# A state-space mixer with a gated FFN on one core: another start for the LayerNorm and the first FFN step

## The chip, the cores and the metric

The kernel runs on one core of a Trainium2 chip. The metric is the device time of one execution in microseconds (us), taken as the median of several runs; lower is better. TensorE (PE in the profile) multiplies matrices, VectorE (DVE) and ScalarE (ACT) work elementwise, GpSimd (POOL) casts weights here and issues some DMAs, SyncE (SP) issues most DMAs. Each engine takes its instructions in the order of the program and waits on semaphores for the others.

## The reference, cut to what matters

The input has 1024 tokens (4 batches of 256) of 512 features. They are normalised once, and two branches read the result:

```python
xn = (x - mean(x)) / sqrt(var(x) + 1e-5)          # per token, over 512 features
s  = mixer(xn)                                    # projections, convolution, decayed state sums, gate, out projection
h  = silu(xn @ gate_w.T) * (xn @ up_w.T)          # FFN, 512 -> 1792
g  = silu(h @ down_w.T)                           # 1792 -> 512
out = x + s * g
```

FFN weights are integers in {-1, 0, 1} with one scale per row. The mixer is by far the larger part.

## The kernel before

Tokens are cut into eight tiles `t` of 128 (`xts[t]`, 128 tokens on the partitions by 512 features). A tile is normalised in place and then turned by TensorE (four 128x128 transposes, `ln_turn`) so that features lie on the partitions. The turned tile is copied by ScalarE into `xnT` (`keep`), which the mixer reads. For the FFN it is also split into a high part `xh` (rounded to the fast matmul type, ScalarE) and a low part `xl` (the rest, VectorE) by `split_tile`; a product with `xh` and one with `xl` together have full precision.

All of the change lies in `front`, which takes the first 300 us of the span. Its main loop runs over 28 FFN steps `(h, f)`: two halves `h` of 512 tokens by 14 tiles `f` of 128 FFN channels. Tiles 0 to 3 are half 0. A step issues, in this order: the loads of a later step's weights (`load_ffn`, three DMAs of 256 KB on SP's queue); the gate product `pg` (eight matmuls of 128x512, `project_exact`); its Silu `sg` on ScalarE; the up product `pu` (eight matmuls); `sg` times `pu` on VectorE (line 584); the next step's weight casts from integer to the matmul type on POOL (`cast_ffn`); the high part `hh` (ScalarE, line 592) and the low part `hl` (VectorE, line 596) of the product; and, two steps late, the down product `pf` (eight matmuls, `down_next`).

Between these calls each step takes three turns of `pieces`, a hand-written list of other work that fills the engines: `first_pieces` normalises and turns tiles 4 to 7, then forms sums of `xnT` for the mixer; from turn 6 on `dt_pieces` runs beside it (two products `pd` of the step sizes, `dt_project(0)` over half 0 and two turns later `dt_project(1)` over half 1, and softplus work); from turn 11 on come the mixer's B and C projections. Nothing is reordered by a scheduler: each engine's order is the order in which the program issues. A tile pool with n buffers makes a new tile wait until the tile n before it is no longer read. Tiles 4 to 7 are turned in a PSUM pool with one buffer (`ps_t`), so a turning waits for the `keep` of the turning before it.

Before the loop, the program loads tiles 0 to 3, step 0's weights, tiles 4 to 7, step 1's weights and small constants, issues eight matmuls `idle` that nobody reads (`busy(8)`), and then walks tiles 0 to 3 in a staggered order:

```python
for t in range(5):
    if t < 4:
        ln_stats(t)
        ln_std(t)
    if t:
        nc.vector.reciprocal(rstd[:, t - 1:t], rstd[:, t - 1:t])
        ln_norm(t - 1)
        tps.append(ln_turn(t - 1))
        busy(4)
    if t > 1:
        split_tile(xh, xl, t - 2, tps[t - 2])
split_tile(xh, xl, 3, tps[3])
```

`ln_stats` is two VectorE instructions (statistics and aggregate), `ln_std` a square root on ScalarE, followed by a reciprocal on VectorE. ScalarE holds one table of functions at a time: Sqrt and Silu are in different tables, and a change of table is an instruction of its own in the profile (ACT_TABLE_LOAD).

Of the kernel before, what the change touches and what calls it, by code (L numbers as in the profile page):

```python
# [43 lines left out]
F32 = mybir.dt.float32  # L44
F32R = mybir.dt.float32r
I32 = mybir.dt.int32
AF = mybir.ActivationFunctionType
ALU = mybir.AluOpType
PSUM = bass.MemoryType.PSUM

P = 128
# [4 lines left out]
NT = T // P  # L56
HID = 512
KT = HID // P
# [3 lines left out]
G = 8  # L62
# [3 lines left out]
CT = DIN // P  # L66
# [7 lines left out]
EPS = 1e-5  # L74
LEAD = 10
EARLY = 10
HALF = T // 2
# [5 lines left out]
def mixer_ffn(ctx: ExitStack, tc: tile.TileContext, x, in_w, conv_w, conv_b, dt_bias, a_log, d_col,  # L83
              norm_w, out_w, gate_t, up_t, down_t, gate_s, up_s, down_s, out):
    nc = tc.nc

    const = ctx.enter_context(tc.tile_pool(name="const", bufs=1))
    small = ctx.enter_context(tc.tile_pool(name="small", bufs=3))
    dram = ctx.enter_context(tc.tile_pool(name="dram", bufs=1, space=bass.MemoryType.DRAM))
    ps_proj = ctx.enter_context(tc.tile_pool(name="ps_proj", bufs=3, space=PSUM))  # L90
# [5 lines left out]
    eps = const.tile([P, 1], F32, name="eps")  # L96
# [5 lines left out]
    tiny = const.tile([P, 1], F32, name="tiny")  # L102
# [29 lines left out]
    def load_w(*tiles):  # L132
        w = wp.tile([P, 2, KT, P], F32, name="w")
        for n, i in enumerate(tiles):
            nc.sync.dma_start(w[:, n], in_w[i])
        return w
# [18 lines left out]
    def combine_w(w):  # L155
        s = scp.tile([P, 3, KT // 2, P], F32, name="s")
        for _ in combine_to(s[:, 0], s[:, 1], s[:, 2], blocks(w)[2], w):
            pass
        return factors(w, s)
# [34 lines left out]
    def front(pre, one_of, fp, f2, hp, ep):  # L194
# [14 lines left out]
        bias = one_of.tile([P, 1], F32, name="bias")  # L209
# [4 lines left out]
        steps = [(h, f) for h in range(2) for f in range(FT)]  # L214
        loads = {}

        def load_ffn(n):
            f, ts = steps[n][1], []
            for tag, src in (("wg", gate_t[f]), ("wu", up_t[f]),
                             ("wd", down_t[f * P:(f + 1) * P, :])):  # L220
                wi = f2.tile([P, HID], I32, name=f"{tag}_i", tag=f"{tag}_i")
                nc.sync.dma_start(wi, src)
                ts.append((tag, wi))
            loads[n] = ts
# [12 lines left out]
        def load_x(ts):  # L237
            for t in ts:
                xt = pre.tile([P, HID], F32, name="xt")
                nc.sync.dma_start(xt, x[t * P:(t + 1) * P, :])  # L240
                xts.append(xt)

        mv = one_of.tile([P, NT, 2], F32, name="mv")
        rstd = one_of.tile([P, NT], F32, name="rstd")
        nc.scalar.activation(rstd[:, 0:1], eps, AF.Sqrt)

        def ln_stats(t):
            st = small.tile([P, 6], F32, name="st")
            nc.vector.bn_stats(st, xts[t])
            nc.vector.bn_aggr(mv[:, t, :], st)  # L250

        def ln_std(t, n=1):
            nc.scalar.activation(rstd[:, t:t + n], mv[:, t:t + n, 1], AF.Sqrt, bias=eps)

        def ln_norm(t):
            nc.vector.tensor_scalar(xts[t], xts[t], mv[:, t, 0:1], rstd[:, t:t + 1],
                                    ALU.subtract, ALU.mult)

        def ln_turn(t):

            p, tag = ((ps_o, "o"), (ps_y, "y"))[t // 2] if t < 4 else (ps_t, "t")
            tp = p.tile([P, KT, P], F32, name="tp", tag=tag)
            for k in range(KT):
                nc.tensor.transpose(tp[:, k, :], xts[t][:, k * P:(k + 1) * P], ident)
            return tp

        def keep(t, tp):
            nc.scalar.copy(xnT[:, :, t * P:(t + 1) * P], tp)

        def busy(n):  # L270

            for _ in range(n):
                nc.tensor.matmul(idle, ones, ones, start=True, stop=True)
# [4 lines left out]
        def split_x():  # L278
            return [hp.tile([P, KT, HALF], F32R, name=n) for n in ("xh", "xl")]

        def split_tile(xh, xl, t, v):
            to = slice(t % 4 * P, (t % 4 + 1) * P)
            nc.scalar.copy(xh[:, :, to], v)
            nc.vector.tensor_tensor(xl[:, :, to], v, xh[:, :, to].bitcast(F32), ALU.subtract)

        def project_exact(w, xh, xl):
            pp = ps_proj.tile([P, HALF], F32, name="pp", tag="proj")
            for k in range(KT):
                for part in (xh, xl):
                    nc.tensor.matmul(pp, w[:, k * P:(k + 1) * P], part[:, k, :],  # L290
                                     start=(k == 0 and part is xh),
                                     stop=(k == KT - 1 and part is xl))
            return pp
# [24 lines left out]
        held = {}  # L318
# [69 lines left out]
        def combine_x(n):  # L388

            a, b = ((x12, x11), (x22, xc[:, 0]), (x22, x12), (x21, xc[:, 1]))[n]  # L390
            nc.vector.tensor_sub(xc[:, n], a, b)

        def first_pieces():
            for t in range(4, NT):
                ln_stats(t)
                if t % 2:
                    yield
            ln_std(4, 4)
            nc.vector.reciprocal(rstd[:, 4:], rstd[:, 4:])
            ln_norm(4)  # L400
            yield
            ln_norm(5)
            yield
            for t in range(4, NT):
                if t + 2 < NT:
                    ln_norm(t + 2)
                keep(t, ln_turn(t))
                yield
            yield
            for n in range(4):  # L410
                combine_x(n)
                if n == 0:
                    held["a"] = combine_w(held.pop("w"))
                yield
# [113 lines left out]
        load_ffn(0)  # L528
        nc.sync.dma_start(gs, gate_s)
        nc.sync.dma_start(us, up_s)  # L530
        load_x(range(4, NT))
        load_ffn(1)
        nc.sync.dma_start(wdt, in_w[PROJ // P - 1])
        nc.sync.dma_start(bias, dt_bias)
        nc.sync.dma_start(a_neg, a_log)
        for to, src in ((cw, conv_w), (cb, conv_b), (dcol, d_col), (nw, norm_w)):
            nc.sync.dma_start(to, src)
        nc.sync.dma_start(ds_bc, down_s.partition_broadcast(P))
        held["w"] = load_w(2 * CT + G, 2 * CT)

        idle = ps_t.tile([P, P], F32, name="idle", tag="t")
        xh, xl = split_x()
        busy(8)
        ws, tps = cast_ffn(0), []
        for t in range(5):
            if t < 4:
                ln_stats(t)
                ln_std(t)
            if t:
                nc.vector.reciprocal(rstd[:, t - 1:t], rstd[:, t - 1:t])  # L550
                ln_norm(t - 1)
                tps.append(ln_turn(t - 1))
                busy(4)
            if t > 1:
                split_tile(xh, xl, t - 2, tps[t - 2])
        split_tile(xh, xl, 3, tps[3])
        for t in range(4):
            keep(t, tps[t])
        pending = []

        def down_next():
# [6 lines left out]

        pfs = None
        for n, (h, f) in enumerate(steps):  # L570
            if n + 2 < len(steps):
                load_ffn(n + 2)
            pg = project_exact(ws[0], xh, xl)
            sg = fp.tile([P, HALF], F32, name="sg")
            nc.scalar.activation(sg, pg, AF.Silu, scale=gs[:, f:f + 1])
            if f == 2 and h:
                ffn_out(h - 1, pfs, (2, 3))
            next(pieces, None)
            pu, wd = project_exact(ws[1], xh, xl), ws[2]
            if f == FT - 1 and h == 0:  # L580
                xh, xl = split_x()
                for t in range(4, NT):
                    split_tile(xh, xl, t, xnT[:, :, t * P:(t + 1) * P])
            nc.vector.scalar_tensor_tensor(sg, pu, us[:, f:f + 1], sg, ALU.mult, ALU.mult)
            if n + 1 < len(steps):
                ws = cast_ffn(n + 1)
            next(pieces, None)
            if len(pending) == 2:
                down_next()
            hh = fp.tile([P, HALF], F32R, name="hh")  # L590
            hl = fp.tile([P, HALF], F32R, name="hl")
            nc.scalar.copy(hh, sg)
            if f == 1 and h:
                ffn_out(h - 1, pfs, (0, 1))
            next(pieces, None)
            nc.vector.tensor_tensor(hl, sg, hh.bitcast(F32), ALU.subtract)
            pending.append((f, hh, hl, wd))
        w = load_w(1, CT + 1)
# [6 lines left out]

    with (tc.manual_schedule(), tc.tile_pool(name="pre", bufs=NT) as pre,
          tc.tile_pool(name="one_of", bufs=1) as one_of, tc.tile_pool(name="fp", bufs=3) as fp,
          tc.tile_pool(name="f2", bufs=2) as f2, tc.tile_pool(name="hp", bufs=1) as hp,
          tc.tile_pool(name="ep", bufs=3) as ep):
        a, w = front(pre, one_of, fp, f2, hp, ep)  # L610

# [211 lines left out]
    with tc.manual_schedule():  # L823
# [4 lines left out]
        for i in range(CT):  # L828
# [32 lines left out]
            if 0 < i < CT - 1:  # L861
                w = load_w(i + 1, CT + i + 1)
# [206 lines left out]
        for n in range(2):  # L1069
            two, to = slice(2 * n, 2 * n + 2), slice(n * HALF, (n + 1) * HALF)  # L1070
# [3 lines left out]
        for n in range(2):  # L1074
            to = slice(n * HALF, (n + 1) * HALF)
# [97 lines left out]
```

## Time and profile before

| | |
|---|---|
| median of 3 runs | 1718.75 us (1718.47 to 1719.07) |
| profiled execution, time | 1718.77 us |
| profiled execution, span from first to last instruction | 1717.1 us |
| PE busy in the span | 1707.1 us |
| DVE, ACT, POOL busy | 1448.4, 1071.3, 217.1 us |
| mean granted TensorE clock | 1.000 |
| first matmul of the FFN starts at | 12.63 us |

The profiled execution's time is its span and 1.67 us around it. Start times are counted from the span's first instruction. A row of the timeline gives the start, the time taken, the engine and line, the operation, what it writes and reads, and in square brackets how long the engine had been idle before it and whom it waited for. The ends of matmuls are modelled, so the pitch between the starts of neighbouring matmuls says more than the time of one.

### The profile page before, as it was taken

The page shows a single profiled execution, that of the slowest core. Times are in us where ns is not written, and L with a number is a line of the kernel's source. Part 1 is how long each engine was busy: PE and PEld are TensorE (multiplying, and loading weights), DVE is VectorE, ACT ScalarE, POOL GpSimd, SP SyncE. Part 2 cuts the span into 40 slices and gives each one's busy share as a digit, 9 for nine tenths or more (in the row PEclk, how much of TensorE's full clock was granted, in tenths as well). Part 3 has the DMA queues.
Part 4 walks back from the last instruction along what each step waited for, and adds up shares of the span by engine and source line. Part 5 has one row for each costly group of instructions (what it writes and reads, how often), then busy time and mean ns, then how long its engine had stood idle before and what let it go on. Part 6 is the DMA issues. An engine that isn't in the chain of part 4 may idle for free.

```text
span 1717.1 us, 22516 instructions
## 1 busy us (share of the span) xinstructions
PE 1707.1 (99%) x8458; PEld 1098.8 (64%) x8458; DVE 1448.4 (84%) x1742; ACT 1071.3 (62%) x1439; POOL 217.1 (13%) x238
## 2 busy tenths in 40 slices
PE   8999999999999999999999999999999999999999
PEld 6666667555566666666666666666666666666687
DVE  5769787788888898889888988898889888899876
ACT  4554333688866666666766676667666666667640
POOL 3223323000000000111011101010111010101110
PEclk9999999999999999999999999999999999999999
DMA  6347665576766666777676767776776676667775
GB/s 227 93 166 251 209 237 201 205 222 209 238 203 205 198 215 175 201 201 205 184 207 197 214 189 211 206 217 194 212 204 203 193 209 195 197 183 210 207 215 182
DMA packets 161931, 347.27 MB, mean 202 GB/s; under 512 B 15136, under 2 KB 52896, under 8 KB 161824
## 3 DMA queue, kind: packets, MB, share of 16 engines
q1 hardware_dynamic: 139136, 292.89, 49.5%
q0 software_dynamic: 22688, 52.96, 17.5%
q8 instruction: 67, 1.10, 0.3%
q14 instruction: 40, 0.33, 0.1%
HBM read 236.48 MB, written 81.00 MB: 185 GB/s over the span
## 4 chain that ended last, share of the span: by engine, by line
PE 96%; DVE 2%; DMA 1%; ACT 0%; issue 0%; SPq 0%; ACTq 0%
PE px L175 29%; PE po L783 22%; PE pq L175 14%; PE py L702 10%; PE pz L175 7%; PE pp L290 5%; PE tp L658 3%; PE pf L298 2%; PE pg L478 1%; DVE cT L183 1%; DMA ya<-gated 0%; PE pd L326 0%; DMA wdt<-in_in_w 0%; DMA wd_i<-in_down_t 0%; DMA w<-in_in_w 0%
## 5 line engine op out<-in xcount | busy, mean ns | idle before, releaser
L175 PE MATMUL px<-xc,w 128*128 128x512 f32 x576 | 271.3, 593 | 0.0
L183 DVE SCALAR_TENSOR_TENSOR xT<-xpad,cw,xT 128x1024 f32<-128x1024 f32 x192 | 246.1, 1282 | 10.0 <-ACT xT L179 5.7
L191 DVE TENSOR_TENSOR_SCAN m<-m,after 128x1024 f32<-128x1024 f32 x108 | 246.4, 2281 | 0.0
L783 PE MATMUL po<-wo,ya 128*128 128x256 f32 x768 | 176.5, 379 | 0.0
L652 DVE TENSOR_TENSOR m<-m,gm 128x1024 f32<-128x1024 f32 x128 | 150.6, 1218 | 15.0 <-ACT m L644 15.0
L702 PE MATMUL py<-m,v 128*64 128x128 f32 x2048 | 160.7, 276 | 0.0
L921 POOL DMA_DIRECT2D sqacc<-sq x54 | 46.1, 853 | 869.5 <-ACT sq L917 805.4
L783 PEld LDWEIGHTS po<-wo,ya 128*128 128x128 f32 x768 | 141.5, 190 | 17.1 <-issue 0.2
L175 PE MATMUL pz<-xnT,w 128*128 128x512 f32 x288 | 145.8, 592 | 0.0
L175 PEld LDWEIGHTS px<-xc,w 128*128 128x128 f32 x576 | 99.3, 190 | 72.2 <-issue 68.9
L175 PE MATMUL px<-xnT,w 128*128 128x512 f32 x288 | 141.8, 615 | 0.0
L175 PE MATMUL pq<-xnT,s 128*128 128x512 f32 x288 | 136.1, 595 | 0.3 <-DVE xpad L951 0.3
L175 PE MATMUL px<-xc,s 128*128 128x512 f32 x288 | 135.7, 593 | 0.6 <-ACT cpad L441 0.5
L175 PE MATMUL pq<-xc,s 128*128 128x512 f32 x288 | 135.3, 592 | 0.0
L644 ACT ACTIVATE m<-m 128x1024 f32<-128x1024 f32 x128 | 134.3, 1058 | 0.6
L658 PEld LDWEIGHTS tp<-ident,xT 128*128 128x128 f32 x512 | 67.8, 141 | 99.4 <-issue 87.6
L702 PEld LDWEIGHTS py<-m,v 128*64 128x64 f32 x2048 | 117.7, 137 | 20.3 <-issue 19.1
L783 PE MATMUL po<-tw,sy 128*128 128x256 f32 x512 | 115.9, 379 | 0.0
L783 PEld LDWEIGHTS po<-tw,sy 128*128 128x128 f32 x512 | 97.2, 190 | 13.2
L891 ACT COPY gT<-px 128x512 f32<-128x512 f32 x64 | 37.5, 586 | 106.0 <-PE px L175 103.1
L702 PE MATMUL py<-mo,v 128*64 128x128 f32 x1024 | 99.7, 273 | 0.0
L175 PEld LDWEIGHTS pq<-xc,s 128*128 128x128 f32 x288 | 54.7, 190 | 68.9 <-issue 62.0
(189 smaller groups left out, 3106.5 us busy)
## 6 DMA issues: line engine op xcount, KB each, us to landing
m<-rows SPq DMA_DIRECT2D x108, 512.0 KB, 6.5
w<-in_in_w SPq DMA_DIRECT2D x144, 256.0 KB, 6.8
mo<-rows SPq DMA_DIRECT2D x128, 256.0 KB, 7.4
gated<-yg SPq DMA_DIRECT2D x64, 512.0 KB, 8.4
ya<-gated SPq DMA_DIRECT2D x30, 1024.0 KB, 7.2
sqacc<-sq POOLq DMA_DIRECT2D x54, 512.0 KB, 6.3
wo<-in_out_w SPq DMA_DIRECT2D x64, 256.0 KB, 6.8
acc<-sa POOLq DMA_DIRECT2D x23, 512.0 KB, 6.0
```

The costliest lines, as they stand in the source:

```text
L175: nc.tensor.matmul(pp, a[:, k, :], b[:, k, :], start=start and k == 0, stop=k == KT // 2 - 1, skip_group_check=not start)
L183: nc.vector.scalar_tensor_tensor(xT, xpad[:, :, k:k + L], cw[:, i, k:k + 1], xT, ALU.mult, ALU.add)
L191: nc.vector.tensor_tensor_scan(m, m, after, 0.0, ALU.add, ALU.mult)
L290: nc.tensor.matmul(pp, w[:, k * P:(k + 1) * P], part[:, k, :], start=(k == 0 and part is xh), stop=(k == KT - 1 and part is xl))
L298: nc.tensor.matmul(pf, part[:, i * P:(i + 1) * P], wd, start=(f == 0 and part is hh), stop=(f == FT - 1 and part is hl))
L644: nc.scalar.activation(m, m, AF.Exp)
L652: nc.vector.tensor_mul(m, m, gm[:, 0:T])
L658: nc.tensor.transpose(tp[:, b, :], xT[:, b, c * P:(c + 1) * P], ident)
L702: nc.tensor.matmul(py[d, q * P:(q + 1) * P], v[:, b, h, :], m, start=False, stop=True, skip_group_check=True)
L783: nc.tensor.matmul(po, a[:, k, :], b[:, k, :], start=start and k == 0, stop=k == HG - 1, skip_group_check=not start)
L891: nc.scalar.copy(gT[:, HALF:], px)
L921: nc.gpsimd.dma_start(sqacc, sq, accum_op=ALU.add)
```

## The change

Six edits, all in `front`:

- Tiles 0 to 3 are normalised one after the other on VectorE before any `xl`; the turnings are issued after that, with `idle` matmuls 12, 4, 4, 2, 2 where there were 8, 4, 4, 4, 4. The Silu table is loaded right after the four `xh`, and two of the four `keep` copies are issued after step 0's Silu.
- Step 0 multiplies the high parts of gate and up first (four and four matmuls) and then the low parts, into two PSUM banks.
- Tiles 4 to 7 get the inverse root on VectorE: a first value from the bits of the number and three Newton steps, twelve instructions on 128x4 elements, for one Sqrt on ScalarE and one reciprocal.
- The turnings of tiles 4 to 7 come one turn later (turns 5 to 8 for 4 to 7); an empty turn behind them goes, so that what follows keeps its turns.
- Weights are loaded three steps ahead for two (`f2` has three buffers for two).
- The order of the first DMAs: step 1's weights before tiles 4 to 7, then step 2's weights, then the mixer's first weight tile `held["w"]`, then the constants.

```diff
-        def ln_std(t, n=1):
-            nc.scalar.activation(rstd[:, t:t + n], mv[:, t:t + n, 1], AF.Sqrt, bias=eps)
+        def ln_std(t):
+            nc.scalar.activation(rstd[:, t:t + 1], mv[:, t, 1:2], AF.Sqrt, bias=eps)
+
+        def ln_inverse(t):
+            nc.vector.reciprocal(rstd[:, t:t + 1], rstd[:, t:t + 1])
...
+        def rstd_begin(to, v):
+            nc.vector.tensor_scalar(v, v, EPS, None, ALU.add)
+            bits = to.bitcast(I32)
+            nc.vector.tensor_scalar(bits, v.bitcast(I32), 1, None, ALU.logical_shift_right)
+            nc.vector.tensor_scalar(bits, bits, -1, 0x5f375a86, ALU.mult, ALU.add)
+
+        def rstd_refine(to, v):
+            y2 = small.tile([P, NT // 2], F32, name="y2")
+            nc.vector.scalar_tensor_tensor(y2, to, -0.5, to, ALU.mult, ALU.mult)
+            nc.vector.tensor_mul(y2, y2, v)
+            nc.vector.scalar_tensor_tensor(to, y2, 1.5, to, ALU.add, ALU.mult)
...
+        def project_part(pp, w, part, first):
+            for k in range(KT):
+                nc.tensor.matmul(pp, w[:, k * P:(k + 1) * P], part[:, k, :],
+                                 start=first and k == 0, stop=not first and k == KT - 1)
...
-            ln_std(4, 4)
-            nc.vector.reciprocal(rstd[:, 4:], rstd[:, 4:])
+            to, v = rstd[:, 4:], mv[:, 4:, 1]
+            rstd_begin(to, v)
+            for _ in range(3):
+                rstd_refine(to, v)
             ln_norm(4)
             yield
             ln_norm(5)
+            yield
             yield
             for t in range(4, NT):
                 if t + 2 < NT:
                     ln_norm(t + 2)
                 keep(t, ln_turn(t))
                 yield
-            yield
...
+        load_ffn(1)
         load_x(range(4, NT))
-        load_ffn(1)
+        load_ffn(2)
+        held["w"] = load_w(2 * CT + G, 2 * CT)
...
-        held["w"] = load_w(2 * CT + G, 2 * CT)
...
-        busy(8)
+        busy(12)
+        for t in range(4):
+            ln_stats(t)
+            ln_std(t)
+            if t:
+                ln_inverse(t - 1)
+                ln_norm(t - 1)
+        ln_inverse(3)
+        ln_norm(3)
         ws, tps = cast_ffn(0), []
...
         for t in range(4):
+            tps.append(ln_turn(t))
+            busy(4 if t < 2 else 2)
+            split_tile(xh, xl, t, tps[t])
+        nc.scalar.activation(tiny, eps, AF.Silu)
+        for t in range(2):
             keep(t, tps[t])
+        first = [proj_bank() for _ in range(2)]
+        for part in (xh, xl):
+            for pp, w in zip(first, ws):
+                project_part(pp, w, part, part is xh)
...
-            if n + 2 < len(steps):
-                load_ffn(n + 2)
-            pg = project_exact(ws[0], xh, xl)
+            if n + 3 < len(steps):
+                load_ffn(n + 3)
+            pg = project_exact(ws[0], xh, xl) if n else first[0]
             sg = fp.tile([P, HALF], F32, name="sg")
             nc.scalar.activation(sg, pg, AF.Silu, scale=gs[:, f:f + 1])
+            if n == 0:
+                for t in range(2, 4):
+                    keep(t, tps[t])
...
-            pu, wd = project_exact(ws[1], xh, xl), ws[2]
+            pu, wd = project_exact(ws[1], xh, xl) if n else first[1], ws[2]
...
-          tc.tile_pool(name="f2", bufs=2) as f2, tc.tile_pool(name="hp", bufs=1) as hp,
+          tc.tile_pool(name="f2", bufs=3) as f2, tc.tile_pool(name="hp", bufs=1) as hp,
```

More of the change, by code (lines that the diff above doesn't have):

```diff
@@ L284, in split_tile, with proj_bank @@
             nc.vector.tensor_tensor(xl[:, :, to], v, xh[:, :, to].bitcast(F32), ALU.subtract)
+        def proj_bank():
+            return ps_proj.tile([P, HALF], F32, name="pp", tag="proj")
+        def project_part(pp, w, part, first):
+            for k in range(KT):
+                nc.tensor.matmul(pp, w[:, k * P:(k + 1) * P], part[:, k, :],
+                                 start=first and k == 0, stop=not first and k == KT - 1)
         def project_exact(w, xh, xl):
-            pp = ps_proj.tile([P, HALF], F32, name="pp", tag="proj")
+            pp = proj_bank()
             for k in range(KT):
@@ L538, in front @@
         nc.sync.dma_start(ds_bc, down_s.partition_broadcast(P))
-        held["w"] = load_w(2 * CT + G, 2 * CT)
         idle = ps_t.tile([P, P], F32, name="idle", tag="t")
         xh, xl = split_x()
-        busy(8)
-        ws, tps = cast_ffn(0), []
[L545 to L556, printed above, removed]
-        for t in range(4):
+        busy(12)
[7 more added lines that the diff above has]
+        ln_norm(3)
+        ws, tps = cast_ffn(0), []
+        for t in range(4):
+            tps.append(ln_turn(t))
[3 more added lines that the diff above has]
+        for t in range(2):
             keep(t, tps[t])
+        first = [proj_bank() for _ in range(2)]
+        for part in (xh, xl):
+            for pp, w in zip(first, ws):
+                project_part(pp, w, part, part is xh)
         pending = []
```

## The prediction

> **What bounds the kernel now.** I read the page's busy shares first, then the busy time by stretches, then PE's waits, then the timelines of PE, DVE and ACT over the first 37 us, which are all that the change touches.
>
> ```profile
> PE 1707.1 (99%) x8458; PEld 1098.8 (64%) x8458; DVE 1448.4 (84%) x1742; ACT 1071.3 (62%) x1439; POOL 217.1 (13%) x238
> ...
> 0.00:40.00 40.00, 35.18 (x166) 26.73 (x167) 22.60 (x44) 17.81 (x30) 13.39 (x30) 1.00 0.69 237
> 40.00:100.00 60.00, 59.89 (x228) 40.12 (x227) 41.55 (x50) 35.12 (x46) 16.57 (x19) 1.00 0.31 86
> ...
> 1700.00:1717.10 17.10, 12.86 (x60) 10.99 (x58) 9.57 (x20) 0.00 (x0) 0.00 (x0) 0.96 0.17 61
> ...
> PE tp L264 <- DVE xt L256: 3.3, 4, 1.2
> PE idle L273 <- POOL ones L196: 1.3, 1, 1.3
> ```
>
> PE is busy for 1707.1 of 1717.1 us. Of the 10.0 us it is idle, 4.8 lie in the first 40 us and 4.2 in the last 17; between them it loses 1 us in 1660. So whatever PE gains or loses before 40 us is passed on whole to the end, and nothing else in the kernel can give much. PE's largest wait is for normalised tiles (line 256), four waits of 3.3 us together. The rows around them:
>
> ```profile
> 11.20 0.66 PE L264 MATMUL tp<-ident,xt 128*128 128x128 f32 x4
> 12.63 0.47 PE L290 MATMUL pp<-xh,wg 128*128 128x512 f32 x1
> 16.81 0.39 PE L290 MATMUL pp<-xh,wg 128*128 128x512 f32 x1
> 21.29 0.63 PE L264 MATMUL tp<-ident,xt 128*128 128x128 f32 x4 [0.69 <-DVE xt L256]
> 23.08 0.63 PE L264 MATMUL tp<-ident,xt 128*128 128x128 f32 x4 [1.16 <-DVE xt L256]
> 33.40 3.60 PE L326 MATMUL pd<-xnT,wdt 128*128 128x512 f32 x8
> ...
> 17.07 0.75 DVE L584 SCALAR_TENSOR_TENSOR sg<-pp,us,sg 128x512 f32<-128x512 f32 x1 [2.26 <-DMA w<-in_in_w]
> 20.12 0.18 DVE L399 RECIPROCAL rstd<-rstd 128x4 f32<-128x4 f32 x1 [0.68 <-ACT rstd L253]
> 20.34 0.81 DVE L256 TENSOR_SCALAR xt<-xt,mv,rstd 128x512 f32<-128x512 f32 x1
> ...
> 11.89 0.59 ACT L283 CAST xh<-tp 128x512 fp32r<-128x512 f32 x1 [0.96 <-PE tp L264]
> 18.50 1.28 ACT L253 ACT_TABLE_LOAD   x1
> 20.11 1.28 ACT L575 ACT_TABLE_LOAD   x1
> 23.63 0.62 ACT L592 CAST hh<-sg 128x512 fp32r<-128x512 f32 x1 [1.06 <-DVE sg L584]
> ```
>
> The last turning of the start (11.20), its `xh` (11.89) and the first product (12.63) form one chain; step 1 begins at 16.81. Then the Sqrt for tiles 4 to 7 waits behind `hh` and a table load (18.50), and tiles 4 and 5 reach PE late (21.29, 23.08). By the chain of waits the second `pd` ends at 36.99, and from there PE runs on. I carry the change's times to that `pd`.
>
> **The start.** Up to the norm of tile 1 (ends 7.43) DVE's order is as before. Then two `xl` (0.69 us each) no longer stand between the norms. Statistics of tile 3 to the norm of tile 2 took 0.99 us (8.07 to 9.06), so that norm starts at 8.4. A norm took 0.55 us alone and 0.72 with a POOL cast beside it; there are casts of step 0 until 8.56 and, since step 1's weights now come first, of step 1 from about 9. With 0.17 for a reciprocal, the norm of tile 3 ends between 9.65 and 10.0; I take 9.9, before 11.15. The turning starts at 9.95, and row 11.20 to row 12.63 puts the first product 1.43 later: 11.4 (11.15 to 11.65 with the other value of the norm and a late `xh`). The twelve `idle` instructions and four Sqrt in ACT's order lie ahead of waits that end later: ACT has the first `xh` ready to start at 8.65 and three take 0.52 each, done by 10.4. The four `xl` take DVE from 9.9 to 12.7; the low products start eight matmuls of 0.227 after 11.4, at 13.2. So high before low hides the `xl` with 0.5 us to spare, and the old 0.16 us wait goes; without that cover each 0.1 us of late `xl` would cost 0.1. Sixteen matmuls of 0.227 us make 3.63: step 1 starts at 15.03 for 16.81, a gain of **1.78 us**.
>
> Three things here I cost at nothing: the Silu table load and four `keep` copies (ACT is free from 11.3 until the gate product ends at 14.3, and after that until 15.9), the constants queued later on SP (the first reader of `wdt` is at 24; issue to landing is 3.6 to 4.7 us), and tiles 4 to 7 loaded behind step 1's weights (issued from about 7.2, landed by 13; read from 12.7 and, tiles 6 and 7, from 16). A queue entry on SP takes 0.45 us, so three moved loads delay tiles 4 to 7 by 1.4 to 2.1 us; if that cover fails, the Newton chain below slips by the same. The third weight buffer changes no wait of PE: PE has none on weights in the whole span.
>
> **Newton.** Before, from the `sg` product at 17.07 to the norm of tile 4 at 20.34 DVE took 3.27 us, of which 0.90 (19.44 to 20.34) are the wait for the Sqrt and the reciprocal. Now the `sg` product is at 17.07 - 1.78 = 15.29, and without those 0.90 the statistics end at 17.66. Twelve dependent instructions on 128x4 follow. The trace has none of their kind; the nearest rows are the 128x1 TENSOR_SCALAR at 0.136 us and the 128x4 RECIPROCAL with 0.22 from its start to the next instruction's. Twelve make 1.63 to 2.64 us; I take 0.136 plus the 0.04 seen between a reciprocal and its norm, 0.18 each and **2.16** in all, as most of them are plain tensor-scalar forms. The norm of tile 4 starts at 19.82, only 0.5 us earlier than before, although the step began 1.78 earlier: two table loads are gone from ACT, but DVE does in its own time what it had waited 0.90 us for. [...]
>
> The turning of tile 4 starts 0.69 us (5.27 to 5.96) to 0.95 (20.34 to 21.29, a cast beside it) after its norm: 20.6. PE has finished step 1 at 15.03 + 3.63 = 18.66, so it waits 1.9 us. Before, by the same pitch, it was done at 16.81 + 3.63 = 20.44 and stood 0.85 us (the row's 0.69 counts from a modelled end).
>
> **Later turnings.** Now step 2's gate product (1.84 us) comes between the turnings of tiles 4 and 5: 21.03 to 22.88. Tile 5's turning must wait for the `keep` of tile 4, which now stands in ACT's order behind `hh` of step 1, and that behind three DVE instructions (norm 4, `hl`, norm 5) and the `sg` product. Norm 4 to `hh` took 3.29 us before (20.34 to 23.63) with casts beside it, and 2.5 at the least (0.55 + 0.68 + 0.55 + 0.75). I take 3.0, plus 1.10 for `hh` and `keep`: 23.9, tile 5 at 23.95, a wait of 1.1 us. What queues behind it on PE: both `pd` and all else. The first `pd` starts at 24.4, where it was 26.00 behind three turnings; of the 1.6 us, 0.44 go again for the turning of tile 6, which comes later.
>
> The turning of tile 7 was issued before a down product, which hid its `keep`. Now it stands right before the second `pd`, which reads that `keep`. Turning to dependent matmul is 1.43 us, of which 0.43 is the turning: a **new wait of 1.0 us** (0.8 to 1.2).
>
> **The sum.** First `pd` 24.4 + 3.44; up product 1.84; turning 0.43; down 1.84; turning and wait 1.43; second `pd` 3.44: it ends at 36.8, before 36.99. The kernel gains 0.2 us. The waits say the same: before, PE stood 0.85 us ahead of tile 4 and 1.36 ahead of tile 5 (21.72 to 23.08), 2.2 together; now 1.9, 1.1 and 1.0, 4.0 together. These 1.8 us more eat the 1.78 of the start, and the 0.2 is what rounding leaves. The profiled execution is at 1718.77, the median at 1718.75: about **1718.5**.
>
> **The rivals.**
>
> 1. *The gain at the start is largely kept.* Newton at its lower bound (-0.53), no casts beside norm 4 to `hh` (-0.5), a first product at 11.2 (-0.2): 1.4 us gained, 1717.3. For it: POOL's casts of step 2 now run near 14 to 16 us and not at 19 to 21. Against: those of step 3 still wait for a DMA issued near 16 and landed near 20.
> 2. *Nothing waits.* With no wait after 11.4 the second `pd` would end at 11.4 + 48 x 0.227 + 4 x 0.43 + 2 x 3.44 + 1.84 = 32.7, 4.2 us earlier: 1714.5. Two orders of instructions speak against it.
> 3. *Slower: the clock.* The first eight `idle` matmuls took 3.78 us (1.34 to 5.12), the next four 1.06, though the granted clock is 1.00 in every row: at first PE runs at half pace. If waits of 1.9 and 1.1 us within 5 us bring that back, one such stretch of 3.78 us costs 1.9: 1720.4. It decides if PE can't bear a wait longer than the 1.16 us that cost it nothing at 23.08 (0.23 pitch right after). [...]
>
> That the change does not do what it says would be an inverse root off the path: then tile 4 waits as above and the time is within 0.5 us of before, inside the forecast.
>
> **How the numbers follow.** About 0.2% (3.4 us) is what a measurement of this kernel can tell from no change. Forecast 0.62; gain kept 0.18; clock 0.12; nothing waits 0.04; two slow stretches or something unseen 0.04. The unknown costs make the forecast's own range 1717.4 to 1719.6 (start 0.25, Newton 0.5, casts 0.45, `keep` 0.2, not all one way); with rivals 1 and 3 it reaches from 1717.0 to 1720.4. Only rival 2 passes 3.4 us of gain, and only something beyond rival 3 passes 3.4 of loss: 0.05 faster, 0.90 the same, 0.05 slower.
>
> **What would show it.** Right: first product near 11.4, step 1 near 15.0, twelve rows of some 0.15 us ending near 19.8, turnings of tiles 4 and 5 near 20.6 and 23.9 with waits of 1.9 and 1.1, 1.0 us of idle PE before the second `pd`, which ends near 36.8. Wrong: a pitch of 0.45 us after 20 us, a second `pd` that ends before 36 or after 38, or a difference that arises after 40 us.

## The result and the profile after

The changed kernel takes 1721.55 us (median of 22 runs, 1720.56 to 1722.28) for 1718.99 of the kernel before beside it (22 runs): a ratio of 1.0014 (95% interval 1.0008 to 1.0020). That is 2.6 us slower: inside the 0.2% that the prediction put down as no change, but 3 us above the forecast and outside its range. Its profiled execution took 1720.83 us with a span of 1719.1, 2.0 more than before.

The page's first part, and the busy time by stretches (stretch, length, then busy us of PE, PEld, DVE, ACT and POOL, granted clock, DMA share, GB/s), of the changed kernel:

```profile
PE 1707.2 (99%) x8458; PEld 1099.5 (64%) x8458; DVE 1450.7 (84%) x1753; ACT 1068.4 (62%) x1437; POOL 212.7 (12%) x238
...
0.00:40.00 40.00, 35.24 (x166) 27.05 (x167) 24.66 (x55) 15.27 (x28) 13.64 (x30) 1.00 0.75 257
...
125.00:300.00 175.00, 172.35 (x699) 119.97 (x698) 142.12 (x144) 66.10 (x92) 48.82 (x45) 1.00 0.60 211
300.00:1700.00 1400.00, 1399.83 (x7204) 883.43 (x7203) 1214.09 (x1464) 940.56 (x1256) 127.15 (x138) 1.00 0.70 206
```

The same stretch of the kernel before, and one line of its list of PE's waits (what PE waited for: us in total, times, longest):

```profile
125.00:300.00 175.00, 174.48 (x709) 122.07 (x708) 143.17 (x146) 66.77 (x93) 53.06 (x45) 1.00 0.63 219
...
PE px L175 <- ACT cpad L441: 0.5, 2, 0.3
```

The first 40 us, where the prediction carried all its sums, are equal: PE is busy for 35.24 us where it was 35.18. PE does its work as before, in 1707.2 us. The whole loss lies between 125 and 300 us, where PE is idle 2.65 us for 0.52: 2.1 us, the difference of the spans. The list of PE's waits in the changed kernel names it:

```profile
PE px L175 <- ACT cpad L466: 2.5, 3, 0.9
PE tp L279 <- DVE xt L259: 2.2, 2, 1.9
...
PE pd L349 <- ACT xnT L283: 0.7, 1, 0.7
```

The wait for normalised tiles is down from 3.3 to 2.2 us, and of the small new ones those before the second `pd` (0.7 us) and for tile 5's turning (0.3) were forecast, at 1.0 and 1.1. But the largest wait is now one that the prediction never spoke of: `px`, a product of the mixer's C projection, waits for `cpad`, the padded tile that ScalarE copies for the convolution. Before it was 0.5 us in two waits; now it is 2.5 in three.

The timelines of the first 37 us (PE, then DVE), against the rows forecast:

```profile
11.70 1.16 PE L306 MATMUL pp<-xh,wg 128*128 128x512 f32 x4 [0.32 <-ACT xh L298]
15.41 0.39 PE L313 MATMUL pp<-xh,wg 128*128 128x512 f32 x1
21.15 0.63 PE L279 MATMUL tp<-ident,xt 128*128 128x128 f32 x4 [1.95 <-DVE xt L259]
23.91 0.66 PE L279 MATMUL tp<-ident,xt 128*128 128x128 f32 x4 [0.29 <-ACT xnT L283]
33.27 3.70 PE L349 MATMUL pd<-xnT,wdt 128*128 128x512 f32 x8 [0.68 <-ACT xnT L283]
...
18.08 0.17 DVE L263 TENSOR_SCALAR mv<-mv 128x4 f32<-128x4 f32 x1
20.46 0.55 DVE L259 TENSOR_SCALAR xt<-xt,mv,rstd 128x512 f32<-128x512 f32 x1
```

First product, step 1, the turnings and the second `pd` (which ends at 36.97 for 36.99 before) all come where the sum put them, within 0.55 us. What follows is about 130 us, not 20.

Around 130 us, the kernel before (POOL's gate-weight cast, then VectorE, then ScalarE):

```profile
131.88 0.61 POOL L230 CAST wg<-wg_i 128x512 fp32r<-128x512 int32 x1 [8.60 <-DMA wg_i<-in_gate_t]
...
128.06 0.67 DVE L596 TENSOR_TENSOR hl<-sg,hh 128x512 fp32r<-128x512 f32 x1
128.93 2.60 DVE L183 SCALAR_TENSOR_TENSOR cT<-cpad,cw,cT 128x1024 f32<-128x1024 f32 x2 [0.21 <-ACT cT L179]
...
133.68 0.59 ACT L441 COPY cpad<-px 128x512 f32<-128x512 f32 x1 [0.83 <-DVE cT L183]
```

The changed kernel, the same place, with ScalarE's and TensorE's rows behind it:

```profile
127.19 1.36 POOL L230 CAST wg<-wg_i 128x512 fp32r<-128x512 int32 x1 [3.90 <-issue]
129.02 0.62 POOL L230 CAST wu<-wu_i 128x512 fp32r<-128x512 int32 x1 [0.47 <-PE pp L313]
130.78 0.61 POOL L230 CAST wd<-wd_i 128x512 fp32r<-128x512 int32 x1 [1.15 <-PE pf L321]
...
125.86 2.28 DVE L191 TENSOR_TENSOR_SCAN em<-em,after 128x1024 f32<-128x1024 f32 x1
128.06 1.03 DVE L630 TENSOR_TENSOR hl<-sg,hh 128x512 fp32r<-128x512 f32 x1
129.02 3.45 DVE L183 SCALAR_TENSOR_TENSOR cT<-cpad,cw,cT 128x1024 f32<-128x1024 f32 x2
...
134.43 0.59 ACT L466 COPY cpad<-px 128x512 f32<-128x512 f32 x1 [0.65 <-DVE cT L183]
...
135.07 1.98 PE L175 MATMUL px<-xc,s 128*128 128x512 f32 x4 [0.80 <-ACT cpad L466]
```

The chain reads downwards. Before, POOL stood idle for 8.60 us until the weights landed, and its cast came at 131.88, when `hl` and the first two taps of the convolution were over. SP issues a gate-weight load at the same moment in both kernels (128.53 and 128.54 us), but with loads three steps ahead it is that of a later step: the weights cast here are long there, and POOL casts as soon as it may, at 127.19. Now the casts of `wg`, `wu` and `wd` lie beside `hl` and the taps, which take 0.36 and 0.85 us longer. The last tap ends later, so ScalarE copies `cpad` at 134.43 for 133.68, and PE waits 0.80 us where it had no listed wait. The same happens at 165.63 (0.87 for 0.28) and 225.55 (0.80 for 0.20): 2.0 us in all.

### The profile page after: what moved, and what is told of

Its sections match the earlier page's. It is cut to its first block, busy times and chain, and to the rows that moved or that the text cites. A ratio compares the mean times of both kernels' runs of the same rounds, so it can differ in the third digit from the quotient of the medians.

```text
span 1719.1 us, 22521 instructions
## 1 busy us (share of the span) xinstructions
PE 1707.2 (99%) x8458; PEld 1099.5 (64%) x8458; DVE 1450.7 (84%) x1753; ACT 1068.4 (62%) x1437; POOL 212.7 (12%) x238
## 4 chain that ended last, share of the span: by engine, by line
PE 95%; DVE 4%; issue 1%; ACT 0%; DMA 0%; ACTq 0%; DVEq 0%
PE px L175 29%; PE po L817 22%; PE pq L175 14%; PE py L736 10%; PE pz L175 7%; PE pp L313 4%; PE tp L692 3%; PE pf L321 2%; DVE cT L183 1%; PE pg L503 1%; DVE em L191 0%; PE pd L349 0%; DVE sg L618 0%; DVE bT L183 0%; PE pp L306 0%
## 5 line engine op out<-in xcount | busy, mean ns | idle before, releaser
L175 PEld LDWEIGHTS px<-xc,s 128*128 128x128 f32 x288 | 54.3, 190 | 69.9 <-issue 63.6
```

The costliest lines, as they stand in the source:

```text
L175: nc.tensor.matmul(pp, a[:, k, :], b[:, k, :], start=start and k == 0, stop=k == KT // 2 - 1, skip_group_check=not start)
```

## The experiments

Three theories were open: (A) the casts that now come early, beside VectorE's operations, cost the time; (B) the earlier DMAs themselves do; (C) the longer wait of PE before tile 4 costs clock in some executions, rival 3 of the prediction. The kernel before was measured again beside each of the four groups of runs: 1719.11, 1719.0, 1719.09 and 1718.88 us.

**Depth alone.** The kernel before with nothing but the deeper loads:

```diff
+        load_ffn(2)
...
-            if n + 2 < len(steps):
-                load_ffn(n + 2)
+            if n + 3 < len(steps):
+                load_ffn(n + 3)
...
-          tc.tile_pool(name="f2", bufs=2) as f2
+          tc.tile_pool(name="f2", bufs=3) as f2
```

> The kernel before with the third weight buffer and loads three steps ahead, nothing else. Theory A (the loss comes from casts on POOL that no longer wait for their weights and run beside VectorE's convolution taps between 130 and 300 us): slower than before by 2.0 to 2.5 us, first product still at 12.6 us, the px matmul near 134 us waits some 0.8 us for the cpad copy, a cast of wg starts near 127 us. Rival C (the new start leaves VectorE behind): within 0.5 us of before.

Measured: 1720.76 us (11 runs), ratio 1.0009 (1.0000 to 1.0018), 1.7 above before and so less than the 2.0 to 2.5 expected. Its list of PE's waits and its busy time by stretches:

```profile
PE px L175 <- ACT cpad L441: 2.4, 3, 0.9
...
125.00:300.00 175.00, 172.37 (x699) 119.83 (x698) 142.24 (x144) 66.09 (x92) 48.47 (x45) 1.00 0.60 210
```

PE is busy for 172.37 us of that stretch, as in the changed kernel (172.35). So this one edit of six makes the loss of that stretch by itself.

**The change without the depth**, and **with the third buffer but loads two steps ahead.** Both take the changed kernel and undo its deeper loads, the first with `bufs=2`, the second with `bufs=3`:

```diff
-        load_ffn(2)
...
-            if n + 3 < len(steps):
-                load_ffn(n + 3)
+            if n + 2 < len(steps):
+                load_ffn(n + 2)
```

> The changed kernel with two weight buffers and loads two steps ahead; the start, Newton and the later turnings stay. Theory A: the second pd ends near 37.0 us as in both kernels, and the time is that of before within 0.5 us, casts of wg near 132 us. Rival C: as slow as the changed kernel, 2 to 2.6 us above before.

> The changed kernel with three weight buffers but loads only two steps ahead: same memory layout as the changed kernel, a load never waits for a cast. Theory A: what counts is when weights land; SP issues a load where the kernel before did or earlier, so casts lie between those of the two kernels: 0 to 1.2 us above before. Rival B (the shifted addresses of the buffers cost the time): as slow as the changed kernel, 2 to 2.6 us above before, whatever the casts do.

Measured: 1719.95 us, ratio 1.0004 (0.9995 to 1.0013), and 1719.90, ratio 1.0004 (0.9996 to 1.0013). In both the `cpad` wait is back at 0.4 us and the two taps at 2.60, and the casts wait for their DMA again (starts at 133.32 and 131.99). The third buffer by itself costs nothing there: PE is busy for 174.44 and 174.51 us between 125 and 300 us. Both medians stay about 0.8 us above before, for the first more than the 0.5 expected; the first trace shows one reason, in the busy time by stretches and PE's timeline:

```profile
20.00:25.00 5.00, 3.63 (x12) 2.92 (x13) 4.93 (x8) 1.11 (x2) 3.92 (x6) 0.69 0.94 344
...
21.37 0.63 PE L279 MATMUL tp<-ident,xt 128*128 128x128 f32 x4 [2.71 <-DVE xt L259]
21.75 0.65 PE L313 MATMUL pp<-xh,wg 128*128 128x512 f32 x1
```

Here tile 4 made PE wait 2.71 us, and the next eight matmuls (the first two at 21.75 and 22.20) go at a pitch of 0.425 us for 0.23, at a granted clock of 0.69 over these 5 us. That is eight times 0.2, or 1.6 us, and the second `pd` starts at 34.56 for 33.27 in the changed kernel. Rival 3 is real, but at 2.71 us; after the 1.95 us of the changed kernel the pitch is 0.23.

**Idle matmuls before tile 4's turning**, in the version with the third buffer and loads two steps ahead:

```diff
             for t in range(4, NT):
                 if t + 2 < NT:
                     ln_norm(t + 2)
+                if t == 4:
+                    busy(8)
                 keep(t, ln_turn(t))
```

> The run with three buffers and loads two steps ahead, whose median was 0.8 us above before while its trace was 0.5 us below, with eight idle matmuls (about 1.9 us) in PE's wait ahead of the turning of tile 4. They add no work that anything waits for. If the wait of 2 us lets PE's clock fall in part of the executions (as the trace of the run without depth shows it at half pace from 21.7 to 25.2 us): the median falls to about 1718.4, 0.5 us below before, and the spread of the times becomes smaller. If the difference is something else: 1719.9 again.

Measured: 1719.52 us, ratio 1.0001 (0.9992 to 1.0010), between the two answers. The idle matmuls fill 18.54 to 20.49 us, and tile 5's turning then waits 0.96 us for a `keep`. Whether the clock falls in some executions after a wait of 2 us is not settled by this.

**More casts on POOL, with loads two steps ahead.** The kernel before, with eight casts of junk that nobody reads ahead of each group's taps, released by the `cpad` tile:

```diff
+            nc.gpsimd.tensor_copy(junk[:, 0:1], cpad[:, 0, TAPS:TAPS + 1])
+            for _ in range(8):
+                nc.gpsimd.tensor_copy(junk, junk_i)
```

> The kernel before (two weight buffers, loads and start as they were) with work on POOL that nobody reads: in each of the eight B/C groups eight casts of 128x512, released when cpad is complete, so that they run beside hl and the first two convolution taps of C on VectorE. No DMA and no load is moved. If POOL's casts as such slow VectorE's taps (theory A): the pair of taps goes from 2.6 to 3.4 us or more, px waits for the cpad copy in most groups, and the time is 2 to 8 us above before. If it is the DMA traffic of the earlier loads: within 0.5 us of before.

Measured: 1722.0 us, ratio 1.0017 (1.0008 to 1.0026), 3.0 above before. PE's largest wait is again the one for `cpad` (list of waits, then the timelines of POOL and VectorE near 130 us):

```profile
PE px L175 <- ACT cpad L444: 3.7, 4, 1.4
...
127.25 0.62 POOL L233 CAST wg<-wg_i 128x512 fp32r<-128x512 int32 x1
...
129.94 1.03 DVE L602 TENSOR_TENSOR hl<-sg,hh 128x512 fp32r<-128x512 f32 x1
```

The eight junk casts hold POOL from 121.95 to 127.25, and so the real ones come beside `hl` (1.03 us again) and the taps (2.95 for the pair, where 3.4 or more was expected). More work on POOL gives the same wait without deeper loads, as theory A says. But the run is coarse: the longest wait, 1.43 us at 167.74, has undisturbed taps (2.58) ahead of it. There the last four junk casts, at 154.75 to 158.41, take 0.92 us each for 0.67 at 121.95, and the addition to `cpad`, which stands behind the four `xl` of the second half in VectorE's order, starts 4.34 us after the product `pq` that it reads (155.20 to 159.54) for 2.80 in the kernel before, so that VectorE comes to the taps 1.5 us late.

**The casts held back, with the deep loads kept.** The reverse: POOL's casts delayed by one-column casts into the tile that the full cast then overwrites. The first try had 24 of them from step 3 on, on the depth-only kernel:

```diff
+                if tag == "wg" and n > 2:
+                    for _ in range(24):
+                        nc.gpsimd.tensor_copy(w[:, 0:1], wi[:, 0:1])
                 nc.gpsimd.tensor_copy(w, wi)
```

> The kernel before with the third buffer and loads three steps ahead (as in the run with the depth alone, 1.65 us above before), but ahead of each cast of wg from step 3 on POOL does 24 casts of one column of the same tile, which hold the real cast back by some 3 to 4 us. Weights land as early as in the run with the depth alone. Theory A: the cast near 127.5 us starts near 131 and no longer lies beside the first two taps of C; of the 2.4 us that px waits there, at least half goes, and the time is at most 1 us above before. If the early landing itself costs the time: still 1.5 to 2.5 us above before.

A miss: 1756.09 us. The narrow casts took far longer than expected (7.91 us for 24 at 126.26), the weights came late, and PE waited 26.7 us for `wg`. With twelve, on the depth-only and on the changed kernel:

> The depth-only kernel (before with the third weight buffer and loads three steps ahead) plus twelve one-column casts on POOL ahead of each gate-weight cast from step 3 on: at the 0.33 us each that 24 of them took, the casts start 4.0 us later, near 131.2 us in the stretch around 130 us for 127.5, while the DMAs stay early. Theory (casts beside the VectorE operations that take both operands from SBUF): the two convolution taps there take about 2.6 us again for 3.45, PE's wait for the cpad copy falls from 2.4 us to 1.0 or less, and the time is within 0.8 us of the kernel before where the depth-only kernel lay 1.5 above. Rival (the earlier DMA traffic itself costs the time): the wait stays at 2 us or more and the time stays 1.2 to 2 above. If weights come late again, a wait of PE for wg or wu of over 1 us shows it.

> The changed kernel plus the same twelve one-column casts ahead of each gate-weight cast from step 3 on. Theory: as for the depth-only kernel, PE's wait for the cpad copy falls from 2.5 us to 1.0 or less, and the time falls to that of the changed kernel with its loads two steps ahead, 0.6 to 1.2 above the kernel before. Rival (earlier DMA traffic): 1.5 to 2.6 above, the wait stays.

Measured: 1721.06 us, ratio 1.0012 (1.0003 to 1.0021), and 1720.73, ratio 1.0010 (1.0001 to 1.0018). The `cpad` wait fell to 0.7 us in both and the pair of taps to 2.61, as theory A said, but the times did not: each has a new wait of 1.8 us for `wg` at the end of the FFN, where its last cast starts at 290 us for 281. By the times alone this would have looked like theory B. So the delay was left out of the first and the last steps:

```diff
-                if tag == "wg" and n > 2:
+                if tag == "wg" and 5 < n < 26:
                     for _ in range(12):
```

> The depth-only kernel with twelve one-column casts ahead of the gate-weight cast of steps 6 to 25 alone, so that the weights of the last two steps aren't late (that wait, 1.8 us, is what the version from step 3 on ended with at 1721.1 for 1719.1 of before). Theory (the time goes where full casts run beside VectorE's taps): PE's wait for the cpad copy stays near 0.7 us, the wait for wg goes, and the profiled span falls by 1.5 to 1.8 from 1719.3 to 1717.5 to 1717.8, a median of 1719.1 to 1719.8, 0 to 0.7 above before. Rival (the earlier DMA traffic, or anything else that the deeper loads bring): 1.2 to 2 us above before, as the depth-only kernel, though the cpad wait is gone.

> The changed kernel with the same twelve one-column casts ahead of the gate-weight cast of steps 6 to 25 alone. Theory: cpad wait 0.7 us or less, no wait for wg, profiled span 1716.9 to 1717.3, a median of 1718.5 to 1719.9 (up to 0.9 above before). Rival: 1.5 to 2.5 us above before.

Measured: 1718.38 us, ratio 0.9995 (0.9986 to 1.0004), for the depth-only kernel, and **1718.65 us, ratio 0.9997 (0.9988 to 1.0005)**, for the changed kernel, both even with before. The second's interval lies clear of 1.0008 to 1.0020, that of the changed kernel. The first came out 0.5 us below before, where 0 to 0.7 above was expected, and its interval overlaps that of the depth-only kernel (1.0000 to 1.0018). Of the changed kernel with the casts held back, the list of waits, the busy time by stretches and the timelines:

```profile
PE px L175 <- ACT cpad L469: 0.7, 1, 0.7
...
125.00:300.00 175.00, 174.17 (x708) 121.79 (x707) 139.04 (x147) 67.05 (x94) 116.69 (x201) 1.00 0.62 215
...
126.63 10.02 POOL L232 CAST wg<-wg_i 128x1 fp32r<-128x1 int32 x12 [3.85 <-PE pp L316]
136.71 1.56 POOL L233 CAST wg<-wg_i 128x512 fp32r<-128x512 int32 x1
...
128.43 2.60 DVE L183 SCALAR_TENSOR_TENSOR cT<-cpad,cw,cT 128x1024 f32<-128x1024 f32 x2 [0.20 <-ACT cT L179]
```

The loads are three steps ahead as in the changed kernel, and SP issues them at the same places in its order (128.04 us here, 0.5 us earlier, as PE is by then). Nothing is removed and POOL's work is even added to, and 1.8 of the 2.1 us between 125 and 300 us are back: the full casts no longer meet the taps, which take 2.60 us. Theory B would have left the time where it was. Theory A holds. The tie with before flatters the change a little, though: the delay also takes a cast away from `hl` at 70 us (1.09 us in both kernels), and PE gains 0.4 us there (`px` at 72.49 for 72.89), so that the span falls by 2.7 us in all, to 1716.4.

**Statistics first.** The traces point to a better version: give tile 4's chain its head start, and leave the loads as they were. All four statistics of tiles 4 to 7 go into the first turn, ahead of step 0's `sg` product on VectorE, and `dt_project(0)` a turn later:

```diff
             for t in range(4, NT):
                 ln_stats(t)
-                if t % 2:
-                    yield
+            yield
+            yield
...
-            for piece, turns in ((lambda: dt_project(0), 2), (lambda: dt_project(1), 1),
-                                 (dt_exp, 3), (dt_ln, 3), (dt_inverse, 1), (dt_softplus, 5),
+            for piece, turns in ((lambda: dt_project(0), 3), (lambda: dt_project(1), 1),
+                                 (dt_exp, 2), (dt_ln, 3), (dt_inverse, 1), (dt_softplus, 5),
```

(with `bufs=2`, loads two steps ahead and no early `load_ffn(2)`).

> The changed kernel with two weight buffers, the statistics of tiles 4 to 7 all ahead of step 0's sg product on VectorE, and the second pd one turn later. If the start's 1.4 us are eaten by the waits for tiles 4, 5 and 7 as the trace shows: the tile 4 turning comes near 19.6 us for 21.15, the wait of 0.7 us before the second pd goes, the second pd ends 2.0 to 2.4 us earlier, and with theory A the time is 2.0 to 2.4 us below before. If VectorE's order cannot give it back, within 0.5 us of before.

Measured: 1716.70 us, ratio 0.9987 (0.9978 to 0.9996). Tile 4's turning waits 0.2 us, but PE now waits 1.9 us for step 2's `wg`, which lands late. The last version takes that away alone: three buffers and step 2's weights in the prologue, behind tiles 4 to 7, while the steps from 1 on still load two ahead:

```diff
         load_x(range(4, NT))
+        load_ffn(2)
...
-            if n + 2 < len(steps):
+            if n and n + 2 < len(steps):
                 load_ffn(n + 2)
```

> The run with early statistics, which was 2.4 us below before, and whose PE waited 1.9 us for step 2's gate weights (cast at 21.3 us because they landed then): step 2's weights are now loaded ahead of the constants into a third buffer, and loads stay two steps ahead after that. Their cast should start near 14.7 us, the wait at 21.97 us should go, and the time is 1.5 to 2.2 us below that run, 3.9 to 4.6 us below before. Rival: the wait for tile 5's turning takes its place; then 0.5 to 1.4 us below that run.

Measured: **1716.19 us (1715.76 to 1717.42), ratio 0.9981 (0.9972 to 0.9990)**, faster than both kernels: 2.8 us below before and 5.4 below the changed kernel. It is short of the 3.9 expected, and 0.5 us below the run before it, as the rival said, though the wait that took the old one's place is tile 4's (0.9 us); the two profiled executions lie 2.0 us apart (spans 1716.3 and 1714.3). The list of waits and PE's timeline:

```profile
PE tp L279 <- DVE xt L259: 0.9, 1, 0.9
...
32.79 3.60 PE L349 MATMUL pd<-xnT,wdt 128*128 128x512 f32 x8
```

The second `pd` starts at 32.79 with step 3's gate product (1.84 us) already done before it, where the changed kernel does that product after it: 0.48 and 1.84 make the 2.3 us that the start gains. The `cpad` wait is 0.5 us, as before, since the casts wait for their loads.

## Why the prediction failed

The step that failed is one sentence, with a cost of nothing: "The third weight buffer changes no wait of PE: PE has none on weights in the whole span." The premise is right and the conclusion doesn't follow. What the runs showed in its place is 2.1 us of idle PE between 125 and 300 us, which that edit makes alone (the depth-only kernel) and which goes for the most part when POOL's casts are held back. Weights that land earlier free no wait of PE, but they free POOL, whose casts had been held back by DMAs. The trace of before showed it in the view of the cast's line (60 to 300 us), under what POOL had been idle for (us, times):

```profile
  DMA wg_i<-in_gate_t: 104.5, 17
```

In the changed kernel this entry is gone, and the casts start when PE lets go of the previous weights. So the question that the prediction did not ask was what a POOL that starts 4.7 us earlier meets. The answer was in the rows of before as well: at 164.30 and 223.65 `px` already waits for `cpad`, 0.28 and 0.20 us. That chain had next to no slack, and most of what VectorE loses ahead of it PE loses too. At the place shown VectorE lost 1.21 us (0.36 and 0.85) and PE 0.80: 0.21 went into a wait for ScalarE that VectorE had there before, and the last tap, now without a cast beside it, took 1.27 us for 1.46. The prediction knew that a cast beside VectorE costs time (it priced a norm at 0.72 us for 0.55), but used it in the first 40 us alone, and its rivals looked for a loss there alone; "a difference that arises after 40 us" stood among the signs of an error, but with no mechanism and no price.

The price could have been bounded from rows of before, where a cast takes 0.61 us undisturbed and 0.74 to 2.49 in company between 130 and 160 us: on the assumption, which no row shows, that a cast holds VectorE up for its own 0.61 us at most, an estimate is between nothing and 1.8 us for the three casts of a step, and at most 5.5 us for the three places, of which the rows of before name two. PE lost 0.80 us at the one shown and 0.6 at each of the others. In the changed kernel's rows both engines lose where they meet: `hl`, the scan before it and the taps read two tensors in SBUF, and the `wg` cast that starts at 127.19 under the scan takes 1.36 us for 0.61 and ends 0.41 us after the scan (128.14), while `hl`, which starts under that cast, takes 1.03 for 0.67. By what mechanism they hold each other up is not shown.

The rest of the sum, point by point:

- **The start**: first product forecast 11.4, measured 11.70; step 1 at 15.03 and 15.41. The gain was 1.40 us for 1.78. The 0.3 us are the norms of tiles 2 and 3, priced at up to 0.72 us each, which took 0.96 and 0.95 beside casts; the low products followed with no wait, as forecast.
- **Newton**: twelve instructions of 0.16 to 0.17 us at a pitch of 0.20, 2.38 in all for 2.16. Only three of them are plain tensor-scalar forms, not most, but all went at the same pitch. Tile 4's norm came at 20.46 for 19.82 and its turning at 21.15 for 20.6; the wait was 1.95 in the row, and 2.11 by the pitch from which 1.9 was forecast.
- **Later turnings**: tile 5's turning at 23.91 for 23.95, which was luck: norm 4 was 0.64 us late, and from it to `hh` took 2.30 us for 3.0. That is below the 2.5 "at the least", which added durations where neighbouring VectorE rows overlap (norm 4 starts 0.46 us before `hl`, not 0.55). The wait came smaller than 1.1, since the product before it was later. The new wait before the second `pd` was 0.68 for 1.0, with 1.28 us from the turning to the `pd` for 1.43. The `pd` ended at 36.97, forecast 36.8.
- **Rival 1** (gain kept): no. **Rival 2**: no. **Rival 3** (clock): not in the changed kernel's trace, but in that of a variant at a wait of 2.71 us.

Of the 3 us by which the forecast missed, 2.0 are these waits and 0.2 the gain that did not come. What stays open is some 0.8 us: the version with shallow loads has a median of 1719.90 though its own profiled execution took 1718.35, and the changed kernel's median is 0.7 above its profiled execution. The clock, as in the variant above, could do that in some executions; no trace of these kernels shows it. The mean granted clocks of the runs hint at it and don't settle it: they lie below 1.000 in 8 of 11 runs of the version with the third buffer and shallow loads, in 3 of 11 with the idle matmuls and in 30 of 102 of the kernel before, but in the first of these such runs are only 0.5 us slower on average than the others.

## What to carry to other kernels

When a transfer is made earlier, follow it past the engine that bounds the kernel: list who waits for it now, and see what that engine will then do earlier and beside whom. Casts on POOL, which take 0.61 us where VectorE is idle (the one at 122.67 in both kernels), lengthened its operations on two tensors in SBUF here by 0.36 us (`hl`) and 0.85 (a pair of taps), and a wait of 0.2 us at the end of such a chain says that there is no slack. To tell contention from transfers, hold back the work and leave the transfer alone, and read the waits as well as the time: a first such kernel was no faster because another wait took the place of the one removed.

## What the runs showed of the hardware

- POOL lost too: in the changed kernel with its casts held back from step 3 on, twelve one-column casts took 10.02 us from 127.33 on, beside VectorE's scan and taps (0.84 each), and 2.90 us (0.24 each) from 91.18 on, where VectorE was idle but for one operation, at 93.76, that reads PSUM.
- After a wait of PE of 2.71 us in mid-stream the granted clock was down, once: 0.69 from 20 to 25 us, with eight matmuls at a pitch of 0.425 us for 0.23. The 2.71 us count from a modelled end; they are 2.87 by the pitch, and 3.25 us pass from product to product if the turning between them isn't counted as work. After 1.95 us (2.49 by that widest count) the pitch stayed at 0.23, and in the version with early statistics after 2.92 so counted. In the run with 24 narrow casts, where PE waited 26.7 us for `wg` in six waits, the longest of 7.0, the granted clock was 0.94 to 0.98 in the stretches between 40 and 330 us.
- One-tensor operations lost too: in the changed kernel the norms of tiles 2 and 3, beside casts, took 0.96 and 0.95 us, those of tiles 0 and 1 0.55. Tile 1's met a cast too, and there the cast lost (0.84 us for 0.61). Which of the two loses can't be told from these starts: tile 3's norm starts at 9.27, before the cast at 9.32, and is the longer one all the same.
